# Moving ten loads of h from SyncE's queue to ScalarE's, and fetching two items ahead in place of five

## The chip, the cores and the metric

The kernel runs on one core of one Trainium2 chip. The metric is device time in microseconds (us) from launch to end. Three runs of the kernel before took 3075.65, 3078.77 and 3074.86 us, so the median is 3075.65 us. Engines are named as in the profile: PE is TensorE (matmuls; PEld its weight loads), DVE is VectorE, ACT is ScalarE, POOL is GpSimd, SP is SyncE. SPq, ACTq and POOLq are the queues on which those engines issue DMAs.

## The reference

Two graph attention layers over N = 2708 nodes with 1024 features, everything in float32; `adj` is an N x N matrix of 0 and 1.

```python
# layer 0
h = relu(layernorm(x))
f = h @ Wf + bf;  g = h @ Wg + bg
e = relu(f @ g.T)
attention = softmax(where(adj > 0, e, -9e15), axis=1)
x = x + attention @ (h @ W + bW)
# layer 1
h = relu(layernorm(x)); hh = h @ W1
e = leaky_relu(hh @ a1 + (hh @ a2).T)
attention = softmax(where(adj > 0, e, -9e15), axis=1)
x = x + relu(attention @ hh)
```

The case concerns layer 0 alone: the score product f @ g.T (the "scores"), and the rows of h that multiply the attention afterwards.

## The kernel before, in words

**Tiling.** The 2708 rows are cut into tiles of 128; 20 of them are worked on as ten pairs, 0 to 9, and a leftover unit (one tile of 128 rows and one of 20). The columns of the score matrix are cut into five panels, p = 0 to 4. Each product of 2 x 2 blocks is done with seven block products instead of eight (Strassen's scheme as Winograd ordered it), named M1 to M7, on sums and differences of blocks.

**The stage around the change: the first scores** (`scores(0, B)`, line 1372). `B` holds the panel's right sides and stays in SBUF. For each pair q the left sides, made earlier, are read from DRAM in four loads of a tile named `As` (line 1391): call them A (for M1 and M6), B (M5, M2), C (M7, M3), each 512 KB, and D (M4), 256 KB. `load` (line 137) puts every one of them on SP's queue in program order. PE's order is M1(q), M4(q-1), M6(q), M5(q), M2(q), M7(q), M3(q), eight matmuls each; M4 of a pair comes after M1 of the next, because `last` runs as the next pair's `left_over`. After pair 9 come the leftover unit's products (lines 1475 and 1483), whose left sides are one `As` load from `hsl_d` (512 KB). Then the next panel's projection starts (`project_q(1)`, matmuls `qx`), from eight loads `hT<-hs_d`, two `hT<-hsl_d`, and the loads of `md`.

DVE empties PSUM between the products, in program order (`nc.hold`). M2, M3, M4 and M7 add onto banks that DVE must have read before.

**The work that is slid in** is a list, `later`. `behind(us)` (line 214) is called after each product and takes items from its front while there is credit. Before `one()` (line 204) runs an item, it calls the fetch of the first `ahead[0]` items in the list, so `ahead` says how many items early the loads start.

**The sums of h** (`sums_h`, line 371) are such items, two for each pair: `first` and `second` hold four DVE operations together (tile `hr`). A pair's fetch makes two loads `hr<-hg_d` of 512 KB each; `first` has the fetch. The sums are stored to `hg_d` by POOL's queue in three stores (512, 256 and 256 KB). They are put into the list at pair q = 8 of the first scores (line 1428). The items of pairs 0 to 3, and `first` of pair 4, run during the rest of the first scores; after the scores `sums_may` stops them until the projection's M1 is done (line 1728). The sums are wanted in layer 0's first aggregation, `attention @ h`.

**Buffers and queues.** `As`, `hr`, `md`, `hc` and the adjacency tiles `adj_i` all come from one pool of 12 buffers (`strm`, line 119). A new tile takes the buffer that was given back longest ago in program order, and its load waits on the queue until that buffer's last use is over: the end of a matmul, of a DVE operation, or, for an `hr` buffer, of the stores that read it. A queue is worked in order: a load that waits holds up all loads behind it. [...]

`by_scalar` (line 540) issues a load on ACT's queue; the kernel before uses it for the rows of W in `prepare_W` alone. The entry `"m"` of `got` is set by `take_max(0)`, in the projection after the first scores.

Of the kernel before, what the change touches and what calls it, by code (L numbers as in the profile page):

```python
# [57 lines left out]
def kernel(  # L58
# [69 lines left out]
    def stream(name, shape=(P, D), dt=FP):  # L128
        return strm.tile(list(shape), dt, tag="strm", name=name)

    def in_16(o, i):

        n = o.shape[0]
        k = n // 16 * 16
        return [(o, i)] if n in (k, 1) or not k or i.shape[0] != n else [(o[:k], i[:k]), (o[k:], i[k:])]

    def load(o, i):
        for a, b in in_16(o, i):
            tc.keep_in_program_order(nc.sync.dma_start(a, b))

    def store(o, i):
        for a, b in in_16(o, i):
            nc.gpsimd.dma_start(a, b)  # L143
# [13 lines left out]
    hg_d = [dram.tile([P, 7, len(g), W], FP, name=f"hg_d{i}") for i, g in enumerate(groups)]  # L157
# [40 lines left out]
    ahead = [5]  # L198
    spare, from_slots = [False], [False]

    def put(us, go, fetch=None, takes_psum=False, ready=None, to=later):
        to.append([us, fetch, go, takes_psum, ready])
# [18 lines left out]
    def held(f, *a):  # L221
        was, nc.hold = nc.hold, ("vector",)
        r = f(*a)
        nc.hold = was
        return r
# [52 lines left out]
    def add(o, a, b):  # L278
        nc.vector.tensor_tensor(o, a, b, OP.add)

    def sub(o, a, b):
        nc.vector.tensor_tensor(o, a, b, OP.subtract)
# [88 lines left out]
    def sums_h():  # L371

        def fetch(q, two):
            i, j = group_of[q]
            for m in (M1, M2):
                two.append(stream("hr", (P, 2, W)))
                load(two[-1], hg_d[i][:, m:m + 2, j])

        def first(q, two):
            (a0, a1), (b0, b1) = ((t[:, 0], t[:, 1]) for t in two)  # L380
            add(b1, a1, b1)
            sub(a1, a0, a1)

        def second(q, two):
            (a0, a1), (b0, b1) = ((t[:, 0], t[:, 1]) for t in two)
            sub(a0, b1, a0)
            sub(b0, b0, a0)
            i, j = group_of[q]
            store(hg_d[i][:, M6:M7 + 1, j], two[0])
            store(hg_d[i][:, M3, j], b0)  # L390
            store(hg_d[i][:, M5, j], b1)
            summed[0] += 1
        for q in range(NQ):
            two = []
            put(1.4, lambda q=q, two=two: held(first, q, two), lambda q=q, two=two: fetch(q, two), ready=lambda: sums_may[0])
            put(1.4, lambda q=q, two=two: held(second, q, two), ready=lambda: sums_may[0])
# [956 lines left out]
    def once(q, k):  # L1353

        return NY if units[q][k] == TINY else P
# [16 lines left out]
    def scores(p, B):  # L1372

        w = width[p]
        h = w // 2
        lo, hi = slice(0, h), slice(h, w)
        fetch, convert, turn = makers[p]
        rb = slot("rb")
        if p == 0:
            spread(rb, columns_of(p, r_[:, first_col[p]:]))  # L1380
        else:
            row_on_all(rb, r_d[p], p)
        acc = slot("acc")
        S = [None] * NT
        rates = (0.8, 1.0, 0.65, 0.65, 0.65)
        lefts = {}

        def product(q, m, ps, start):
            n, i = P, BY_SCORES.index(m)
            if i % 2 == 0:  # L1390
                t = stream("As", (P, 2, NH, P))
                lefts[q] = t
                k = min(2, 7 - i)
                load(t[:, :k].rearrange("p m c j -> p (m c j)"),
                     hs_d[q][:, i:i + k].rearrange("p m c j -> p (m c j)"))
            for c in range(NH):
                nc.tensor.matmul(ps[:n, :h], lefts[q][:, i % 2, c, :n], B[m][c // 2][:, c % 2, :h],  # L1397
                                 start=(start and c == 0), stop=(c == NH - 1), skip_group_check=True)

        def finish(q, s, k):  # L1400

            n, mk = once(q, k), mk_sb[p, q]
            nc.vector.scalar_tensor_tensor(s[:, :w], s[:, :w], 0.0, mk[:, k, :w], op0=OP.max, op1=OP.add)
            if q == 0 and k == 0:
                nc.vector.tensor_copy(acc[:, :w], s[:, :w])
            else:
                nc.vector.tensor_tensor(acc[:n, :w], acc[:n, :w], s[:n, :w], OP.max)
            if q in known:
                raise_max(p, q, k, mk[:n, k, :w])

        def last(q, sb, Z, m1):

            n = P
            product(q, M4, Z, False)
            add(sb[:n, lo], Z[:n, :h], m1[:n, lo])
            finish(q, sb, 1)
            mk_sb.pop((p, q))
            behind(rate, True)

        nc.hold = ("vector",)  # L1420
        left_over = None
        for q in range(NQ):
            n = P
            make_until(q + 2)
            rate = 1.3 if NQ - 1 not in made else rates[p]
            if q + 2 <= LEFT:
                fetch(q + 2)
            if p == 0 and q == NQ - 2:
                sums_h()
            if p in ORDERED and q in (2, 6):  # L1430
                (copy_residual if q == 2 else bias_residual)(p)
            sa, sb = slot("Sa"), slot("Sb")
            S[pairs[q][0]], S[pairs[q][1]] = sa, sb
            X, Y, Z = (bank(f"s{k}") for k in "xyz")
            m1, t = slot("sm1"), slot("st")
            product(q, M1, X, True)
            for s in (lo, hi):
                add(m1[:n, s], X[:n, :h], rb[:n, s])
            if left_over:
                left_over()  # L1440
            product(q, M6, Z, True)
            add(t[:n, lo], Z[:n, :h], m1[:n, hi])
            behind(rate, True)
            product(q, M5, Y, True)
            add(t[:n, hi], Y[:n, :h], m1[:n, hi])
            if q + 1 <= LEFT:
                convert(q + 1, p > 0)
            behind(rate, True)
            product(q, M2, X, False)
            add(sa[:n, lo], X[:n, :h], rb[:n, lo])  # L1450
            if q + 1 <= LEFT:
                turn(q + 1, 0)
            behind(rate, True)
            product(q, M7, Z, False)
            add(sb[:n, hi], Z[:n, :h], t[:n, hi])
            if q + 1 <= LEFT:
                turn(q + 1, 1)
            behind(rate, True)
            product(q, M3, Y, False)
            add(sa[:n, hi], Y[:n, :h], t[:n, lo])  # L1460
            finish(q, sa, 0)
            behind(2 * rate, True)
            left_over = lambda q=q, sb=sb, Z=Z, m1=m1: last(q, sb, Z, m1)

        sums_may[0] = False
        sm, st = slot("Sa"), slot("Sb")
        S[MONO], S[TINY] = sm, st
        X, Y, Z = (bank(f"s{k}") for k in "xyz")
        m1, zs = slot("sm1"), slot("sz")
        t = stream("As", (P, 2, NH, P))  # L1470
        load(t.rearrange("p e c j -> p (e c j)"), hsl_d.rearrange("p e c j -> p (e c j)"))

        def part(ps, e, m, start):
            for c in range(NH):
                nc.tensor.matmul(ps[:, :h], t[:, e, c], B[m][c // 2][:, c % 2, :h], start=(start and c == 0),
                                 stop=(c == NH - 1), skip_group_check=True)
        part(X, 0, M1, True)
        add(m1[:, hi], X[:, :h], rb[:, hi])
        left_over()

        for c in range(NH):
            for g, (e, m) in enumerate(((0, M1), (1, M2), (0, M5), (1, M3))):
                nc.tensor.matmul(Z[B32 * g:B32 * (g + 1), :h], tinyT[:, e, c], B[m][c // 2][:, c % 2, :h], start=(c == 0),
                                 stop=(c == NH - 1), skip_group_check=True)
        nc.scalar.copy(zs[:, :h], Z[:, :h])
        part(X, 1, M2, False)
        add(sm[:, lo], X[:, :h], rb[:, lo])
        behind(rate, True)
        part(Y, 0, M5, True)
        part(Y, 1, M3, False)  # L1490
        add(sm[:, hi], Y[:, :h], m1[:, hi])
        finish(LEFT, sm, 0)
        for s, pick in zip((lo, hi), picks):
            V = bank("sv")
            nc.tensor.matmul(V[:, :h], pick, zs[:, :h], start=True, stop=True)
            add(st[:, s], V[:, :h], rb[:, s])
        finish(LEFT, st, 1)
        mk_sb.pop((p, LEFT))
        behind(rate, True)
        nc.hold = ()  # L1500
        return S, acc
# [189 lines left out]
    got = {}  # L1691
# [205 lines left out]
```

## Time and profile before

| | us |
|---|---|
| median of three runs | 3075.65 |
| the profiled execution's own time | 3071.02 |
| its span | 3069.2 |
| PE busy | 2999.9 (98%) |
| DVE busy | 2042.9 (67%) |
| ACT busy | 546.1 (18%) |
| first scores, from pair 8's M5 to the first matmul of the projection | 340.68 to 391.14 |

The profile page gives busy time by engine, DMA by queue, the chain of work that ended last, and groups of equal instructions. The trace behind it answers for any stretch of time: an engine's instructions in order with what ended the idle time before them, the issues on a DMA queue, and busy time, clock and DMA share by stretches. All times in the span are counted from its start.

### The profile page before, as it was taken

The page shows a single profiled execution, that of the slowest core. Times are in us where ns is not written, and L with a number is a line of the kernel's source. Part 1 is how long each engine was busy: PE and PEld are TensorE (multiplying, and loading weights), DVE is VectorE, ACT ScalarE, POOL GpSimd, SP SyncE. Part 2 cuts the span into 40 slices and gives each one's busy share as a digit, 9 for nine tenths or more (in the row PEclk, how much of TensorE's full clock was granted, in tenths as well). Part 3 has the DMA queues.
Part 4 walks back from the last instruction along what each step waited for, and adds up shares of the span by engine and source line. Part 5 has one row for each costly group of instructions (what it writes and reads, how often), then busy time and mean ns, then how long its engine had stood idle before and what let it go on. Part 6 is the DMA issues. An engine that isn't in the chain of part 4 may idle for free.

```text
span 3069.2 us, 41688 instructions
## 1 busy us (share of the span) xinstructions
PE 2999.9 (98%) x14630; PEld 2298.9 (75%) x14630; DVE 2042.9 (67%) x4577; ACT 546.1 (18%) x887; POOL 496.0 (16%) x770
## 2 busy tenths in 40 slices
PE   8998899999999999999999999998999999999999
PEld 4576677757877588885888887784767969879695
DVE  5776694676651586715965266967868767887863
ACT  3420020021110121101211011202222121222200
POOL 1421101210011110214102011131212011020201
PEclk9999999999999999999999999998999999999999
DMA  6989868897565786758967588689767868878897
GB/s 227 301 258 274 291 239 294 275 291 222 178 234 152 228 254 221 247 154 238 280 216 250 165 234 264 230 293 332 240 212 249 274 201 302 279 271 295 259 300 270
DMA packets 448065, 766.80 MB, mean 250 GB/s; under 512 B 175488, under 2 KB 262304, under 8 KB 447824
## 3 DMA queue, kind: packets, MB, share of 16 engines
q1 hardware_dynamic: 390416, 590.05, 60.2%
q0 software_dynamic: 54464, 164.78, 16.1%
q10 hardware_dynamic: 2976, 9.31, 0.9%
q8 instruction: 116, 1.90, 0.2%
q14 instruction: 93, 0.76, 0.1%
HBM read 630.04 MB, written 138.11 MB: 250 GB/s over the span
## 4 chain that ended last, share of the span: by engine, by line
PE 75%; DVE 9%; issue 7%; DMA 6%; POOL 1%; SPq 1%; ACT 1%; POOLq 0%; DVEq 0%; ACTq 0%
PE gy L673 7%; PE sz L1397 7%; PE gz L673 7%; PE gx L673 6%; PE gz L1086 5%; PE sx L1397 4%; PE sy L1397 4%; PE px L1286 4%; PE pz L1286 4%; PE py L1286 3%; PE gx L1086 3%; PE gy L1086 3%; PE gv L673 3%; PE M_ps L586 3%; PE qz L673 2%
## 5 line engine op out<-in xcount | busy, mean ns | idle before, releaser
L1397 PE MATMUL sz<-B,As 128*128 128x288 f32 (+2 forms) x1200 | 294.3, 395 | 5.9 <-DVE st L45 4.5
L1397 PEld LDWEIGHTS sz<-B,As 128*128 128x128 f32 x1200 | 229.1, 192 | 56.6 <-DVE st L45 8.2
L1397 PE MATMUL sx<-B,As 128*128 128x288 f32 (+2 forms) x800 | 203.6, 398 | 16.5 <-DMA As<-hs_d 14.6
L1397 PE MATMUL sy<-B,As 128*128 128x288 f32 (+2 forms) x800 | 199.0, 392 | 0.0
L1397 PEld LDWEIGHTS sx<-B,As 128*128 128x128 f32 x800 | 153.5, 193 | 51.2 <-DMA As<-hs_d 12.9
L673 PE MATMUL gz<-Sa,hc 128*128 128x288 f32 (+2 forms) x800 | 185.8, 392 | 0.0
L673 PEld LDWEIGHTS gz<-Sa,hc 128*128 128x128 f32 x800 | 151.5, 190 | 32.2 <-issue 2.2
L1397 PEld LDWEIGHTS sy<-B,As 128*128 128x128 f32 x800 | 151.7, 190 | 30.6 <-DVE st L45 0.3
L1086 PE MATMUL gz<-quarter,hc 128*128 128x128 f32 (+2 forms) x1344 | 168.8, 279 | 3.8 <-DVE gT L45 3.7
L1086 PEld LDWEIGHTS gz<-quarter,hc 128*128 128x128 f32 x1344 | 160.6, 191 | 5.1 <-DVE gT L45 4.6
L143 POOL DMA_DIRECT2D out_dram<-x_res x164 | 80.9, 500 | 467.2 <-DVE x_res L45 456.6
L1286 PE MATMUL px<-w,gT 128*128 128x512 f32 x320 | 141.2, 593 | 1.5 <-ACT pt L45 1.5
L1286 PE MATMUL py<-w,ps 128*128 128x512 f32 x320 | 142.2, 593 | 0.0
L1286 PE MATMUL pz<-w,ps 128*128 128x512 f32 x320 | 142.1, 594 | 0.0
L143 POOL DMA_DIRECT2D mk_d<-mask x55 | 35.9, 653 | 510.7 <-DVE mask L45 504.8
L673 PE MATMUL gy<-T,hc 128*128 128x288 f32 (+2 forms) x480 | 113.6, 398 | 3.9 <-DMA hc<-hg_d 3.9
L1286 PEld LDWEIGHTS pz<-w,ps 128*128 128x128 f32 x320 | 60.2, 190 | 76.2 <-issue 70.3
L1286 PEld LDWEIGHTS py<-w,ps 128*128 128x128 f32 x320 | 60.5, 190 | 75.1 <-issue 72.0
L1286 PEld LDWEIGHTS px<-w,gT 128*128 128x128 f32 x320 | 60.1, 190 | 72.9 <-issue 66.9
L586 PE MATMUL M_ps<-wgT,wfT 128*128 128x512 f32 x256 | 111.8, 593 | 1.6 <-ACT hsT L45 1.6
L673 PEld LDWEIGHTS gy<-T,hc 128*128 128x128 f32 x480 | 92.2, 192 | 24.4 <-DMA hc<-hg_d 4.4
L45 ACT ACTIVATE P<-P 128x576 f32<-128x576 f32 (+2 forms) x110 | 71.9, 654 | 207.6 <-DVE P L45 207.5
(384 smaller groups left out, 5829.1 us busy)
## 6 DMA issues: line engine op xcount, KB each, us to landing
hc<-hg_d SPq DMA_DIRECT2D x175, 512.0 KB
As<-hs_d SPq DMA_DIRECT2D x150, 512.0 KB
hc<-hr_d SPq DMA_DIRECT2D x119, 512.0 KB
hc<-hs_d SPq DMA_DIRECT2D x112, 512.0 KB
w<-wt_d SPq DMA_DIRECT2D x96, 512.0 KB
w<-in_L_gnn_W_dram SPq DMA_DIRECT2D x72, 512.0 KB
md<-md_d SPq DMA_DIRECT2D x56, 512.0 KB
adj_i<-in_adj_dram SPq DMA_DIRECT2D x200, 128.0 KB
```

Of the source, the lines that this page charges most:

```text
L45: i = f(*a, **k)
L143: nc.gpsimd.dma_start(a, b)
L586: nc.tensor.matmul(ps, wfT[a][c // NH][:, c % NH, :], wgT[b][c], start=(c == 0), stop=(c == NC - 1))
L673: nc.tensor.matmul(ps[d], left(m, k, d), right(m, k), start=(start and k == 0), stop=(k == K - 1), skip_group_check=True)
L1086: nc.tensor.matmul(ps[:, d], lhs[:, d * P:(d + 1) * P], inner_right(m, n, k), start=(start and k == 0 and d == 0), stop=(k == NK - 1), ski ...
L1286: nc.tensor.matmul(ps, left[i][m][:, k, :], w_[k], start=(start and k == 0), stop=(k == NH - 1), skip_group_check=True)
L1397: nc.tensor.matmul(ps[:n, :h], lefts[q][:, i % 2, c, :n], B[m][c // 2][:, c % 2, :h], start=(start and c == 0), stop=(c == NH - 1), skip_g ...
```

## The change

Two edits. In `sums_h` the loads of `hr` go through `by_scalar` as long as `"m"` is not in `got`, and through `load` after that. And `ahead` is set to 2 where the sums are put into the list; it was 5 until the end of the first scores, where the kernel before sets it to 2 as well.

```diff
@@ def sums_h(): def fetch(q, two):
             for m in (M1, M2):
                 two.append(stream("hr", (P, 2, W)))
-                load(two[-1], hg_d[i][:, m:m + 2, j])
+                (load if "m" in got else by_scalar)(two[-1], hg_d[i][:, m:m + 2, j])
@@ def scores(p, B):
             if p == 0 and q == NQ - 2:
+                ahead[0] = 2
                 sums_h()
```

In the built kernel, ten of the twenty `hr` loads (pairs 0 to 4) are issued by ACT; they stand after the last copies `hsT<-h_ps` and ahead of the copy `sz<-sz` of the leftover unit. The other ten stay with SP. Before, SP's queue held the `hr` loads of pairs 0 to 6 among the `As` loads of pairs 8 and 9; now it holds none there, and those of pairs 5 to 7 stand together after the projection's first four `md` loads, where before only those of pair 7 stood. Fewer `hr` loads ahead also means that other buffers of the pool come round for the `As` loads. The order of instructions on PE, DVE and POOL is the same in both kernels.

## The prediction

> **What bounds the kernel now.** I began with the page: PE carries the time, so only what keeps PE waiting or slow counts.
>
> ```profile
> PE 2999.9 (98%) x14630; PEld 2298.9 (75%) x14630; DVE 2042.9 (67%) x4577; ACT 546.1 (18%) x887; POOL 496.0 (16%) x770
> ```
>
> Next I took the stage of the change in stretches of 5 us (PE busy, PEld, DVE, ACT, POOL, PE clock, DMA share, GB/s).
>
> ```profile
> 335.00:340.00 5.00, 5.00 (x23) 3.90 (x22) 3.73 (x7) 0.00 (x0) 0.16 (x1) 1.00 0.70 249
> 345.00:350.00 5.00, 3.99 (x16) 2.96 (x16) 4.42 (x11) 0.00 (x0) 0.82 (x2) 1.00 0.68 238
> 350.00:355.00 5.00, 0.13 (x1) 0.00 (x0) 3.87 (x6) 0.00 (x0) 2.09 (x4) 0.87 1.00 313
> 355.00:360.00 5.00, 4.70 (x10) 3.41 (x11) 0.46 (x2) 0.00 (x0) 0.00 (x0) 0.50 1.00 394
> 370.00:375.00 5.00, 1.70 (x7) 0.98 (x6) 4.86 (x10) 0.00 (x0) 1.82 (x3) 0.91 1.00 374
> 375.00:380.00 5.00, 4.70 (x10) 3.42 (x11) 1.03 (x2) 0.00 (x0) 0.54 (x1) 0.50 1.10 370
> 395.00:400.00 5.00, 5.00 (x25) 3.99 (x24) 3.63 (x8) 1.20 (x3) 0.00 (x0) 1.00 0.16 22
> ```
>
> PE nearly stops twice, and runs at half clock after each stop. The chain of work (start, us) says for what:
>
> ```profile
> 340.87 5.00 DMA As<-hs_d
> 346.01 2.19 PE sz L1397 x8
> 348.91 6.34 DMA As<-hs_d
> 355.30 4.21 PE sx L1397 x8
> ...
> 367.85 7.41 DMA As<-hsl_d
> ...
> 375.30 4.21 PE sx L1475 x8
> 379.51 2.73 PE sz L1397 x8
> ```
>
> Three `As` loads come late: C of pair 8, A of pair 9, the leftover's. SP's queue in the same stretch shows why they were issued late:
>
> ```profile
> 347.88 0.94 SPq L139 DMA_DIRECT2D hr<-hg_d  x2
> 348.91 1.68 SPq L139 DMA_DIRECT2D As<-hs_d  x3
> 359.52 2.88 SPq L139 DMA_DIRECT2D hr<-hg_d  x2
> 362.50 0.41 SPq L139 DMA_DIRECT2D As<-hs_d  x1
> 363.97 3.40 SPq L139 DMA_DIRECT2D hr<-hg_d  x2
> 367.85 0.52 SPq L139 DMA_DIRECT2D As<-hsl_d  x1
> ```
>
> Ahead of each stand `hr` loads that wait for buffers; SP's waits from 300 to 480 by what ended them (us in all, times, the longest) say which:
>
> ```profile
> SPq L139 <- DMA hg_d<-hr: 48.2, 14, 8.9
> ```
>
> So the queue stood for stores of finished sums.
>
> The loss: eight matmuls take 1.94 us from start to start here. From 340.68 to 391.14 lie 16 such groups, the leftover's small products (2.07) and four picks (0.97): 34.1 us of work in 50.5, so **16.4 us lost**. Group by group: 1.45 before 346.01, 5.34 before 355.30, 3.77 before 375.30, and 5.8 in slowed matmuls (4.00 for 1.94 twice, the rest just after).
>
> [...] the clock is 0.50 after the stops of 5.17 and 3.60 us, and after one of 1.29 the eight matmuls take 2.18. [...] the share is 1.00 with SP and POOL issuing. [...]
>
> **The change, part by part.**
>
> *Removed:* fourteen `hr` loads from among the `As` loads on SP. Each took about 0.36 us to issue, which is nothing; what counted was their waiting.
>
> *Added:* ten `hr` loads on ACT, 0.33 us each by the rows of W that ACT's queue already loads. ACT stood idle for 127.4 us until 384.38, and behind them is only the copy `sz<-sz`, after the last `hr` load's condition (M4 of pair 8) by 15 us of products. Cost: 0. Without that idle time it would be 3.3 us plus the waits.
>
> *Moved:* four `hr` loads (pairs 5 and 6) now go out after the first scores: 2 MB less in the crowded stretch, about 5.5 us at the 370 GB/s seen when full. They wait on SP ahead of `md` for the third product, but that `md` waits for the projection's M1 to end anyway. The last of these loads waits for the end of the leftover's products, T (the projection's start); six loads of 0.5 MB are 8.5 us of transfer, begun about 7 us before T, landing by about T+5. DVE wants pair 5 at about T+11.5 (402.7 against 391.1). Hidden with 6 us to spare; beyond those, each us late is a us of DVE, which is busy all of 410 to 450.
>
> [...]
>
> *Walking PE without stalls*, from the built kernel's waits (the load's condition, the time by the row before, and when PE wants it):
> - A of 9: M4 of pair 7 ends at 338.7, lands by 345, wanted 348.4.
> - D of 8: M6 of 8, 340.7, lands by 346, wanted 350.4.
> - B of 9: now waits for pair 0's store of 512 KB. That store was done at 347.87 before (the `hr` load behind it went out then). Two ACT loads now run beside it from 344.6, 1 MB, at half share: 1 to 1.5 us later, 349.0. Landing takes 5.0 to 6.34: 354.0 to 355.4, wanted 354.3. I take **0.7 late**.
> - C of 9: right behind it, lands by 357.5, wanted 358.1. In time.
> - Leftover: waits for pair 1's store. Before, issued at about 350.9, done at 359.5. The bytes in 348.5 to 357.5 are about as many (3.3 MB against 3.1), but the `hr` loads are now on another queue; I take 357.6 to 358. Landing 5.0 to 6.3: 363.5, wanted 362.0 plus the 0.7. **0.8 late**.
> - D of 9: just behind, wanted 1.9 later still. In time.
> - `hT` and `md`: before, from the first `hT` issue (371.64) to the last of the four `md` issues is 13.5 us, and about 4 to land (3.93 by a quiet `md`): 17. From 358.7 that is 376; PE wants them at 374.8 plus 1.5. I take **0.8 late** as the midpoint of 0 and 1.6.
>
> *DVE under a PE that doesn't stall:* pair 8 with six sums operations extra carries about 15.2 us of DVE work in a 13.6 us period. It falls about 3.5 us behind by 357.5. PE wants M6's bank read 3.9 us after M6 ends, so this just fits. With 0.4 us to spare I count 0, with 1 us in the range.
>
> Sum: 16.4 - 0.7 - 0.8 - 0.8 = **14.1 us gained**. [...] On the profiled execution: 3071.02 - 14.1 = 3056.9; it lies 4.63 below the median, so the forecast is **3061.6**. After T, PE has one wait on DMA (3.9 us, `hc<-hg_d`), which hangs on DVE and stores that shift with T, so nothing gives the gain back.
>
> **Rivals.**
> 1. *Stores gate the leftover* (one real stop stays). The slowest rows: pair 1's store done at 359.5, landing 7.41 us: 366.9, so 4.9 late, plus 3.1 of half clock, plus 1.4 for B of 9. Loss 9.4, gain 7.0: 3068.7. For: DMA share 1.00. Against: less to move.
> 2. *DMA is the limit, whichever queue.* Before T about 12.7 MB must move from 338.8 on (`As` 2.5, `hr` 2, stores of sums 4.2, masks 0.9, `hT` 2.2, `md` 1). At the 322 GB/s mean of 340 to 390 that is 39.4 us, 378.2 against 374.8: gain 13. At 254 GB/s, 50 us and nothing is gained: about 3075. The 228 to 246 GB/s of 280 to 320 speak for it, but those hold the small adjacency pieces, which end at 322.
> 3. *Slower:* [...] each `As` load lands as late as the slowest row of W on ACT's queue, 11.3 us (median 7.9). A of 9 is 1.7 late, B of 9 4.3 more and 2.9 of clock, the leftover (pair 1's store as late again) 3.4 and 3.1, `hT` and `md` about 4: 19.4 lost, 3 more than now. It decides from about 10.5 us of landing; at 13, some 9 us slower: 3084. Against: 0.5 MB takes 5.0 to 7.4 here with as much beside it.
> 4. *It doesn't do what it says:* ten of twenty loads only are moved. But those are all that stand among the `As` loads, so this is not a case of its own.
>
> **How the numbers follow.** The likeliest case (gain 10 to 16.4) 0.66; rival 1 (5 to 10) 0.16; rival 2 (within 5) 0.12; rival 3 0.06. A measurement of this kernel tells about 0.2%, 6.2 us. Faster by more is the first and most of the second, 0.81; within 0.13; slower 0.06. The range takes the first two cases: from 3057.5 (all of 16.4, and 1.8 for the runs' spread) to 3070.5.
>
> **What would show it.** Right: ACT's queue holds ten `hr` loads between 323 and 353; no wait of PE above 2 us and no clock of 0.50 between 340 and T; T near 377 in place of 391.14; DVE's run of ten `hr` operations starts about 11 us after T, as before. Wrong: `As<-hsl_d` issued after 360, or landing in over 7 us; a clock of 0.50; `hr` waits of DVE after T; T earlier, but a new wait of PE before 500.

## The result, and the profile after

The kernel after takes **3064.88 us** (median of 6 runs, 3062.58 to 3065.96); the kernel before took 3075.28 us beside it (6 runs, 3070.99 to 3079.16). The comparison gives a ratio of 0.9956 with a 95% interval of 0.9947 to 0.9966; the quotient of the two medians is 0.9966, a gain of 10.4 us. The forecast was 3061.6 with a range of 3057.5 to 3070.5.

On the profile page PE is still the engine that carries the time, with 7.3 us less than before:

```profile
PE 2992.6 (98%) x14630; PEld 2293.3 (75%) x14630; DVE 2041.7 (67%) x4577; ACT 546.0 (18%) x887; POOL 496.2 (16%) x770
```

The stage of the change in stretches of 5 us (the columns are as before: PE, PEld, DVE, ACT and POOL busy, clock, DMA share, GB/s):

```profile
340.00:345.00 5.00, 5.00 (x22) 3.95 (x21) 3.96 (x6) 0.00 (x0) 0.54 (x1) 1.00 0.53 168
350.00:355.00 5.00, 5.00 (x22) 3.90 (x21) 4.86 (x9) 0.00 (x0) 1.94 (x4) 1.00 1.02 365
355.00:360.00 5.00, 4.57 (x19) 3.32 (x18) 4.90 (x11) 0.00 (x0) 1.53 (x3) 1.00 1.01 383
365.00:370.00 5.00, 2.46 (x10) 1.99 (x11) 4.02 (x7) 0.00 (x0) 1.98 (x4) 1.00 1.05 351
375.00:380.00 5.00, 5.00 (x22) 3.94 (x21) 0.64 (x2) 0.00 (x0) 0.00 (x0) 1.00 1.12 348
```

The clock is 1.00 in every stretch, and one stretch is left in which PE does half of what it could. PE's timeline names its stop (start, us, what, and in brackets the idle time before and what ended it):

```profile
342.64 2.10 PE L1397 MATMUL sy<-B,As 128*128 128x288 f32 x8
...
356.81 2.21 PE L1397 MATMUL sy<-B,As 128*128 128x288 f32 x8 [0.43 <-DMA As<-hs_d]
...
367.54 2.21 PE L1476 MATMUL sx<-B,As 128*128 128x288 f32 x8 [2.70 <-DMA As<-hsl_d]
...
380.59 7.92 PE L673 MATMUL qx<-hT,md 128*128 128x288 f32 x32
```

342.64 is M5 of pair 8 and 380.59 the projection's start, T. The stage takes 37.95 us in place of 50.46. C of pair 8 and A of pair 9 are on time; B of 9 and the leftover's load are late by 0.43 and 2.70 us. SP's queue and ACT's in the same stretch:

```profile
323.90 26.73 SPq L139 DMA_DIRECT2D As<-hs_d  x8
360.83 0.32 SPq L139 DMA_DIRECT2D As<-hsl_d  x1
361.77 0.32 SPq L139 DMA_DIRECT2D As<-hs_d  x1
362.14 10.82 SPq L139 DMA_DIRECT2D hT<-hs_d  x8
373.00 2.01 SPq L139 DMA_DIRECT2D hT<-hsl_d  x2
375.12 2.53 SPq L139 DMA_DIRECT2D md<-md_d  x4
377.77 4.58 SPq L139 DMA_DIRECT2D hr<-hg_d  x6
```

```profile
322.27 32.61 ACTq L45 DMA_DIRECT2D hr<-hg_d  x10
```

No `hr` load stands among the `As` loads any more. Yet SP's waits from 300 to 480, by what ended them (us in all, times, the longest), hardly differ from the 48.2 us in 14 waits of before:

```profile
SPq L139 <- DMA hg_d<-hr: 44.8, 14, 10.1
```

SP stands for stores nearly as long; the longest of these waits is now that of `As<-hsl_d` itself. That the waiting stayed and the time went was the first hint that the queue was not the matter.

### The profile page after: what moved, and what is told of

Same layout as the page of the kernel before. It is cut to its first block, busy times and chain, and to the rows that moved or that the text cites. A ratio compares the mean times of both kernels' runs of the same rounds, so it can differ in the third digit from the quotient of the medians.

```text
span 3060.8 us, 41690 instructions
## 1 busy us (share of the span) xinstructions
PE 2992.6 (98%) x14630; PEld 2293.3 (75%) x14630; DVE 2041.7 (67%) x4577; ACT 546.0 (18%) x887; POOL 496.2 (16%) x770
## 4 chain that ended last, share of the span: by engine, by line
PE 71%; issue 11%; DVE 9%; DMA 4%; POOL 2%; SPq 1%; ACT 1%; POOLq 0%; DVEq 0%; ACTq 0%
PE gy L673 7%; PE gx L673 6%; PE gz L673 6%; PE sz L1397 6%; PE gz L1086 5%; PE pz L1286 4%; PE px L1286 4%; PE sx L1397 4%; PE sy L1397 3%; PE py L1286 3%; PE gy L1086 3%; PE gx L1086 3%; PE M_ps L586 3%; PE gv L673 2%; PE qz L673 2%
## 5 line engine op out<-in xcount | busy, mean ns | idle before, releaser
L1397 PEld LDWEIGHTS sx<-B,As 128*128 128x128 f32 x800 | 152.4, 191 | 48.4 <-DMA As<-hs_d 10.4
```

## The experiments

Every kernel has the same order of matmuls but for one place in `all_slots`, so one reading serves all: the *head* up to M5 of pair 8, the *stage* from there to T, and the *tail* from T to the end of the span, all from PE's timeline.

| run | head | stage | tail | median us (runs) | ratio to before [95%] |
|---|---|---|---|---|---|
| before | 340.68 | 50.46 | 2678.06 | | |
| before_look | 346.62 | 50.40 | 2680.38 | one run | |
| after | 342.64 | 37.95 | 2680.21 | 3064.88 (6) | 0.9956 [0.9947, 0.9966] |
| again | 343.87 | 39.24 | 2677.89 | 3065.59 (7) | 0.9972 [0.9961, 0.9983] |
| again2 | 348.52 | 39.27 | 2678.91 | 3068.45 (5) | 0.9958 [0.9946, 0.9971] |
| queue_only | 345.37 | 49.05 | 2679.78 | 3072.95 (13) | 0.9998 [0.9990, 1.0007] |
| ahead_only | 345.95 | 38.87 | 2679.08 | 3064.14 (6) | 0.9969 [0.9958, 0.9981] |
| left_slots | 344.95 | 36.80 | 2680.15 | 3063.70 (5) | 0.9962 [0.9950, 0.9975] |
| pool16_before | 342.94 | 40.00 | 2702.76 | 3089.14 (5) | 1.0043 [1.0028, 1.0057] |
| pool14_after | 338.12 | 34.67 | 2697.01 | 3069.32 (19) | 0.9980 [0.9973, 0.9987] |
| act_all | 346.91 | 40.85 | 2694.04 | 3076.55 (12) | 1.0005 [0.9996, 1.0013] |
| ahead3 | 343.48 | 42.78 | 2682.64 | 3070.59 (9) | 0.9971 [0.9961, 0.9981] |
| ahead1 | 350.89 | 38.55 | 2682.46 | 3072.30 (6) | 0.9972 [0.9961, 0.9983] |
| all_slots | 343.85 | 38.84 | 2680.21 | 3064.68 (5) | 0.9951 [0.9937, 0.9964] |

The kernel before took 3073.24 us beside again, queue_only, ahead_only and left_slots (20 runs), 3075.32 beside before_look, pool16_before, pool14_after and act_all (32), and 3080.96 beside the last four (15); so times compare only within a group, stages across all. The head spreads over 13 us, and over 10 us without the two pool kernels, in which alone the program differs long before the head ends; that is about the spread of single times of the kernel before (3069.19 to 3081.10 in the 32 runs).

**Each edit alone.** The two edits of the change, one at a time, and the whole change again.

```diff
# queue_only
-                load(two[-1], hg_d[i][:, m:m + 2, j])
+                (load if "m" in got else by_scalar)(two[-1], hg_d[i][:, m:m + 2, j])
# ahead_only
             if p == 0 and q == NQ - 2:
+                ahead[0] = 2
                 sums_h()
```

> The changed kernel once more, for a closer interval and a second profile. By the walk corrected with its first profile (stage from pair 8's M5 to the projection 37.95 us against 50.46) it is 12.5 us faster than before; by the medians of its first runs 10.4. If the 2 us between them are given back later in the kernel, the stage is again 12 to 13 us shorter and the whole only 10; if they are spread from elsewhere, the two agree within 2 us over more runs. The leftover's As load again waits for pair 1's store and PE for it by 2 to 4 us.

> Only the first edit: hr loads by ACT's queue, still five items ahead. Theory (two causes: the queue's order, and how many hr tiles hold buffers): the hr loads no longer stand before the As loads, but six hr tiles still hold half of the pool, so As loads themselves wait for the stores of sums: D of pair 8 for pair 0's, C of pair 9 for pair 1's, D of pair 9 for pair 2's. About 1.4 late for C of 8, 0.8 for A of 9, 2.5, 3 and 1 for those three: 9 us lost of which before lost 16.4, so a gain of 4 to 8 us (about 3070). Rival (the queue alone is the cause): nearly the whole gain of the change, 9 to 13 us, and no As load issued within 0.5 us of a store's landing.

> Only the second edit: two items ahead, all hr loads still on SP. Theory: this is the larger part. Two hr loads (pairs 3 and 4) still stand before As loads, the last of them waiting for pair 1's store with the leftover's As load behind it, so that load goes out at the same time as in the changed kernel (about 18 us after pair 8's M5 began) and lands 0 to 1.5 us later behind 0.5 MB more on its own queue. A gain of 8 to 12 us (3063 to 3067), at most 3 short of the whole change. Rival (the queue alone is the cause): a gain under 4 us.

The whole change repeats, but the stage of again is 11.2 us shorter than before, not 12 to 13: after its stop of 3.00 us the next two groups of eight matmuls took 2.89 and 2.88 us from start to start in place of 1.94. The edit of `ahead` alone gives all of it, with every `hr` load still on SP. The edit of the queue alone gives nothing clear of the noise: the interval holds 1, and the 4 to 8 us that I expected of it were wrong. PE's timeline of queue_only:

```profile
350.12 2.18 PE L1397 MATMUL sz<-B,As 128*128 128x288 f32 x8 [0.71 <-DMA As<-hs_d]
...
357.20 2.21 PE L1397 MATMUL sx<-B,As 128*128 128x288 f32 x8 [2.96 <-DMA As<-hs_d]
362.34 5.81 PE L1397 MATMUL sz<-B,As 128*128 128x288 f32 x16 [2.93 <-DMA As<-hs_d]
...
379.69 3.90 PE L1475 MATMUL sx<-B,As 128*128 128x288 f32 x8 [3.78 <-DMA As<-hsl_d]
```

and its two queues, SP's first, then ACT's, and two rows of what SP waited for from 300 to 480 us (us in all, times, the longest):

```profile
323.10 41.37 SPq L139 DMA_DIRECT2D As<-hs_d  x8
372.05 0.32 SPq L139 DMA_DIRECT2D As<-hsl_d  x1
```

```profile
321.82 49.76 ACTq L45 DMA_DIRECT2D hr<-hg_d  x14
```

```profile
SPq L139 <- PE sx L1397: 15.9, 4, 7.4
SPq L139 <- PE sz L1397: 9.3, 1, 9.3
```

The fourteen `hr` loads are off SP's queue, and the eight `As` loads still take 41.37 us to go out, against 26.73 in the kernel after. The `As` loads' own conditions say why. When each went out, in us from the start of M5 of pair 8, and what ended its wait, from the traces:

| load | before | queue_only | its wait in queue_only ended with | after | its wait in after ended with |
|---|---|---|---|---|---|
| C of 8 | 0.2 | 0.2 | M6 of 8 | -10.4 | DVE (an adjacency tile) |
| A of 9 | 8.2 | 4.1 | M2 of 8 | -1.8 | M4 of 7 |
| D of 8 | 8.8 | 10.2 | a store of pair 0 | 0.2 | M6 of 8 |
| B of 9 | 9.5 | 10.6 | (behind D of 8) | 5.8 | a store of pair 0 |
| C of 9 | 21.8 | 18.8 | a store of pair 1 | 7.7 | a store of pair 0 |
| leftover | 27.2 | 26.7 | M2 of 9 | 18.2 | a store of pair 1 |
| D of 9 | 30.6 | 29.6 | a store of pair 2 | 19.1 | a store of pair 1 |

PE stops in queue_only for C of 8, A of 9, D of 8 and the leftover's load. Only one of these, D of 8, waited for a store. The other three were dealt the buffer of an `As` tile used just before: M6 is the last product that reads A of its pair, M2 the last that reads B. So such a load can go out only two products, 3.9 us, before it is wanted itself. With fourteen `hr` tiles fetched early from a pool of 12, so few buffers are left that an `As` load takes over that of the `As` tile two or three loads before it. With ten, C of 8 and A of 9 meet buffers that came free earlier, and so does the leftover's load, though that one waits for a store.

**Buffers, bytes or queue.** The kernel before, its queue and its loads untouched, with four more buffers in the pool; and once more as it is, to see whether the 50.46 repeats.

```diff
# pool16_before
-    slots = ctx.enter_context(tc.tile_pool(name="slots", bufs=54))
-    strm = ctx.enter_context(tc.tile_pool(name="strm", bufs=12))
+    slots = ctx.enter_context(tc.tile_pool(name="slots", bufs=47))
+    strm = ctx.enter_context(tc.tile_pool(name="strm", bufs=16))
```

> The kernel before, once more. The stage is counted from pair 8's M5 to the first matmul of the next projection; the head is what lies before it, the tail what lies after it to the end of the span. If the program repeats itself, the stage takes 49.5 to 51.5 us (50.46 in the first profile) with the same three stops, for C of pair 8, A of pair 9 and the leftover; the head lies in 340 to 346 and the tail in 2677.5 to 2680.5, where those of all profiles so far lie. If the 50.46 was an accident of one run, the stage comes out below 45 us and the whole comparison of stages falls.

> The kernel before (all loads on SyncE, five items ahead, so the same bytes and the same queue), with the streaming pool at 16 buffers in place of 12 and 47 slots in place of 54. With four more buffers the As loads of pairs 8 and 9 meet buffers that matmuls and DVE give back, except B of 9 (pair 0's store) and the leftover (behind an hr load that waits for pair 1's store): the same two conditions as in the changed kernel. My theory now (buffers, not the queue and not the bytes): no stop at C of 8 or A of 9, the stage falls from 50.5 to 38 to 42 us, and the kernel is 8 to 12 us faster than before, 3063 to 3067, with ten hr loads still on SyncE. Rival, bandwidth: the 2 MB that the changed kernel leaves out of the stretch are what counts; here they are still in it, so the stage stays at 45 us or more and the gain is under 6 us. Rival, the queue of SyncE itself: as before, stage 49 to 51 us, no gain.

The stage repeats at 50.40 (only the head, 346.62, lies past what I gave it). With 16 buffers it takes 40.00. PE's timeline of pool16_before has these stops and no others in the stage:

```profile
363.37 3.71 PE L1397 MATMUL sz<-B,As 128*128 128x288 f32 x8 [2.80 <-DMA As<-hs_d]
...
369.90 2.21 PE L1475 MATMUL sx<-B,As 128*128 128x288 f32 x8 [0.88 <-DMA As<-hsl_d]
```

and its SP queue still holds the `hr` loads in the midst of the `As` loads:

```profile
334.70 2.97 SPq L139 DMA_DIRECT2D hr<-hg_d  x2
341.20 9.84 SPq L139 DMA_DIRECT2D As<-hs_d  x3
351.30 0.88 SPq L139 DMA_DIRECT2D hr<-hg_d  x2
352.29 0.41 SPq L139 DMA_DIRECT2D As<-hs_d  x1
353.12 8.69 SPq L139 DMA_DIRECT2D hr<-hg_d  x2
361.92 0.45 SPq L139 DMA_DIRECT2D As<-hsl_d  x1
```

So 10.4 of the 11.6 us that the change saves in the stage (mean of after, again and again2: 38.8) come with more buffers alone, the queue as it was and nearly all of the bytes: from 20.6 us ahead of the stage to T, 21.1 MB are moved here, 22.1 in the kernel before and 19.0 in the kernel after. The forecast of the total, 8 to 12 us faster, failed all the same: the tail grew by 22 us or more (from 1200 to 2400 PE is busy 1163 us, against 1182 in the kernel before). My reading is that the stages after T miss the seven tiles that the other pool gave up; no run takes these away by themselves. That does not touch the reading of the stage.

**Taking the last stop away.** Four ways to free the leftover's load from pair 1's store: its left sides in tiles of the other pool (left_slots); those and two loads of pair 9 (all_slots); 14 buffers in the pool (pool14_after); three items ahead, which happens to deal the leftover a buffer that a matmul gives back (ahead3). The last edit has its counterpart in ahead1.

```diff
# left_slots (all_slots does the same for B and D of pair 9)
-        t = stream("As", (P, 2, NH, P))
-        load(t.rearrange("p e c j -> p (e c j)"), hsl_d.rearrange("p e c j -> p (e c j)"))
+        if p == 0:
+            sides = [slot("Asl", (P, NH, P)) for _ in range(2)]
+            for e in range(2):
+                load(sides[e].rearrange("p c j -> p (c j)"), hsl_d[:, e].rearrange("p c j -> p (c j)"))
...
# pool14_after
-    slots = ctx.enter_context(tc.tile_pool(name="slots", bufs=54))
-    strm = ctx.enter_context(tc.tile_pool(name="strm", bufs=12))
+    slots = ctx.enter_context(tc.tile_pool(name="slots", bufs=51))
+    strm = ctx.enter_context(tc.tile_pool(name="strm", bufs=14))
# ahead3
-                ahead[0] = 2
+                ahead[0] = 3
                 sums_h()
# ahead1
-                ahead[0] = 2
+                ahead[0] = 1
                 sums_h()
```

> The changed kernel, with the leftover's left sides in two tiles of the other pool (slots) for the first panel, so that their loads wait for no store. Theory (the 2.7 us wait of PE is the store that gates the load, not DMA bandwidth): the load goes out 9 to 10 us earlier, right behind C of pair 9, and PE's wait for the leftover goes; D of pair 9 keeps the gate and may be up to 1 us late. 2 to 3 us faster than the changed kernel, about 14 to 15 faster than before. Rival (bandwidth): the same bytes move in the same time, so the wait returns at D of pair 9 or at the projection's first hT or md, and the time is that of the changed kernel within 1 us.

> The changed kernel with 14 streaming buffers and 51 slots. No As load of pairs 8, 9 or the leftover waits for a store any more; only matmuls and DVE give their buffers back, and two hr loads on ScalarE wait for pair 0's stores. Theory (stores that hold buffers are all that is left to gain): the wait of 2.7 to 3.0 us before the leftover's products goes, the stage takes 34.5 to 36.5 us against 38.0 and 39.2, and the kernel is 2 to 4 us faster than the changed one, 3060 to 3063. Rival, bandwidth: the loads go out earlier and land slower, the wait comes back at the projection's first matmul (1 to 3 us), and the time stays at 3063 to 3066.

> The changed kernel with three loads for pair 9 and the leftover (B and D of 9, the leftover's left sides) read into tiles of the other pool, each split in two, so that none of them waits for a store; C of 9 waits for pair 0's stores. Sizes of both pools as they were. Theory: stage 34.5 to 36.5 us, the kernel 1.5 to 4 us faster than the changed one on this chip, as long as the tiles taken from the other pool make nothing wait elsewhere (the part after T stays within 2677.5 to 2680.5). Rival, bandwidth: the earlier loads collide, and 1 to 3 us come back at the projection's first matmul.

> The changed kernel with three items ahead in place of two. Twelve hr loads then go to ScalarE and eight to SyncE, 1 MB more is read ahead of the projection, and the pool comes round otherwise: the leftover's load waits for the end of M6 of pair 9, some ten us ahead of the leftover's products, not for pair 1's store; D of 9 for a product too; of the As loads only B of 9 still waits for a store (pair 0's first). Theory (what counts is which loads take over buffers that stores hold): the wait of 2.7 to 3.0 us before the leftover's products goes although more is read, the stage from pair 8's M5 to the projection takes 34.5 to 37 us, and the kernel is 1 to 3 us faster than the changed one on this chip. Rival (fewer hr loads ahead is what helps, by their bytes): three lies between five and two, the stage takes 40 to 45 us and the kernel is 2 to 5 us slower than the changed one.

> The changed kernel with one item ahead in place of two. Ten hr loads on ScalarE still, but they start later. By the buffers, C of 9 waits for pair 0's stores and the leftover's load and D of 9 for pair 1's, much as in the changed kernel. Theory: the leftover is late as before by 2 to 4 us, the sums' operands may come late on DVE (under 2 us each), the stage takes 37.5 to 42 us and the kernel is within 3 us of the changed one, on the slower side. Rival (fewer bytes ahead help): stage below 37 us, 1 to 3 us faster than the changed one.

> The changed kernel once more, on the chip of the three runs beside it: stage 37.5 to 40 us, part after T 2677.5 to 2680.5, time 8 to 12 us below the kernel before on the same chip. It is the measure for the other three, nothing else.

The leftover's wait goes in all of left_slots, all_slots, pool14_after and ahead3. In left_slots 1.25 us return at D of 9, which still waits for pair 1's store, and 0.85 at the projection; the stage is 2.4 us shorter than that of again. In pool14_after nothing takes its place; the stage is 34.67 us, within 0.6 of the 34.1 of pure work. Its PE timeline around T:

```profile
371.93 0.65 PE L1496 MATMUL sv<-sz,pick_hi 128*128 128x288 f32 x2
372.79 8.37 PE L673 MATMUL qx<-hT,md 128*128 128x288 f32 x32 [0.21 <-issue]
```

But with three tiles less in the other pool the tail is 17 to 19 us longer, and by its ratio the kernel gains less than the changed one. In all_slots C of 9 is 0.40 us late, PE waits 0.98 us for DVE where the order of products differs, and the projection's `hT` and `md` are late, as the rival said:

```profile
379.34 0.65 PE L1507 MATMUL sv<-sz,pick_hi 128*128 128x288 f32 x2
382.69 8.00 PE L673 MATMUL qx<-hT,md 128*128 128x288 f32 x32 [2.70 <-issue]
```

("issue" here: this view names no releaser; by the trace the first `md` load, out at 377.63, landed at 382.60.) In ahead3 my forecast fell, and stage and time are those of the rival. A of 9 is late, and the projection too:

```profile
345.42 2.10 PE L1397 MATMUL sx<-B,As 128*128 128x288 f32 x8
...
353.44 3.90 PE L1397 MATMUL sx<-B,As 128*128 128x288 f32 x8 [2.04 <-DMA As<-hs_d]
...
386.26 9.84 PE L673 MATMUL qx<-hT,md 128*128 128x288 f32 x32 [3.19 <-issue]
```

But the first of these stops is not one of bytes. A of 9 went out at 347.55, right when M2 of pair 8 (345.42, above) had ended, and landed in 5.9 us: as in queue_only it was dealt the buffer of B of 8. I had looked for stores alone. For the projection, `hT` stands on the queue behind D of 9, which went out at 365.12 when M2 of 9 had ended, and the `hT` loads then took 12.67 us to go out, 10.82 in the kernel after. How much of the 3.19 us is crowding, no run separates. With twelve early `hr` loads in place of ten, the DMA share is higher where the kernel after leaves room:

```profile
340.00:350.00 10.00, 10.00 (x43) 7.82 (x42) 8.69 (x17) 0.00 (x0) 2.37 (x4) 1.00 1.05 400
```

400 GB/s at a share of 1.05 from 340 to 350, against 212 at 0.64 in the kernel after. Yet pool16_before moves as much to T (21.1 MB, 20.9 here) in a stage 2.8 us shorter. Where the leftover's load is early (left_slots, all_slots), part of the stop returns at the projection. That the transfers crowd each other there is my reading; no run takes bytes away there alone. By their medians left_slots and all_slots lie 1.9 and 3.8 us below the changed kernel on their chips; their intervals overlap its, so no version is shown to beat it. ahead1 stays close to the changed kernel in the stage (38.55, leftover 2.40 and projection 1.26 late), so fewer bytes ahead did not help as its rival had it. It is 3.9 us slower by its median, of which about 3 us lie in the tail; why there, I did not look for.

**Without the cover for the moved loads.** The prediction held six `hr` loads after T to be hidden. Here all twenty go to ACT, and those of pairs 5 to 7 then stand behind ACT's evictions of the projection.

```diff
-                (load if "m" in got else by_scalar)(two[-1], hg_d[i][:, m:m + 2, j])
+                by_scalar(two[-1], hg_d[i][:, m:m + 2, j])
```

> The changed kernel with all twenty hr loads on ScalarE. Those of pairs 5 to 7 then stand among ScalarE's evictions of the projection, behind its first one (some 9 us after T, the projection's start), where on SyncE they were issued by about T + 2. The prediction called the loads of pairs 5 and 6 hidden with 6 us to spare. If that margin is right, pair 5's operations on DVE begin 2 to 6 us later than T + 10.5 and DVE, busy there, ends its sums that much later; TensorE loses 0 to 3 us in the projection, and the kernel takes 3065 to 3068, still 7 us below the kernel before. If the margin is larger than I thought, nothing changes (3063 to 3066). If the waits on ScalarE's queue hold up the evictions that TensorE needs, over 3 us are lost: 3069 or more. The stage before T is as in the changed kernel, 37 to 40 us, in every case.

The loads go out some 13 us later, counted from T (from T + 10.6, where the kernel after has T - 2.8). The timelines of act_all: ACT's queue, DVE, and PE.

```profile
398.35 2.19 ACTq L45 DMA_DIRECT2D hr<-hg_d  x4
402.17 1.00 ACTq L45 DMA_DIRECT2D hr<-hg_d  x2
```

```profile
406.59 0.69 DVE L45 TENSOR_TENSOR hr<-hr 128x512 f32<-128x512 f32 x1 [7.60 <-DMA hr<-hg_d]
...
417.44 0.69 DVE L45 TENSOR_TENSOR hr<-hr 128x512 f32<-128x512 f32 x1 [3.03 <-DMA hr<-hg_d]
```

```profile
444.93 10.20 PE L673 MATMUL qz<-hT,md 128*128 128x288 f32 x32 [7.23 <-DVE B L45]
```

(The kernel after has ten `hr` operations in one run at 391.13, T + 10.5.) The margin lay near where I thought: the loads are 13.4 us later and DVE waits 7.6 for pair 5, so 5.8 were to spare, but 7.6 is past the 2 to 6 expected. The price did not: DVE stands 10.6 us in all, PE 8.1 for DVE (this stop and one of 0.88) and then runs slowed (10.20 us for the 32 matmuls, 8.01 for the 32 before them; clock 0.66 from 440 to 450), and the tail is 14 us or more longer, against 0 to 3 expected. The profiled run is the slowest of the twelve, 7.0 us above their median. The third of my branches, waits worth over 3 us, came about by another road than ACT's evictions. The stage was to stay at 37 to 40 us and took 40.85: a stop of 3.40 at the leftover, and slowed matmuls after it (4.21 us for eight; clock 0.66 from 370 to 380). The whole gain is gone. In this program SP's place behind the first `md` loads is needed.

## Why the prediction was right, and where it was not

- *Removed:* "what counted was their waiting". This is the step that failed: queue_only takes the `hr` loads off SP's queue and keeps 49.05 us. Of the three late loads in the kernel before, only A of 9 (348.91) stood behind an `hr` load that waited for a store, until 347.88. C of 8 went out at 340.87 and the leftover's load at 367.85, each right at the end of the product that gave its own buffer back, M6 of 8 and M2 of 9. PE's timeline of the kernel before (M6 of 8 is the second half of the first row):

```profile
336.80 4.04 PE L1397 MATMUL sz<-B,As 128*128 128x288 f32 x16
...
365.71 2.10 PE L1397 MATMUL sx<-B,As 128*128 128x288 f32 x8
```

The forecast came near because the walk used the load conditions of the built kernel after, where these buffers come free earlier; the sentence about the cause named the wrong part of the change. The edit that does it is the one of `ahead`, which I booked under "moved" and "2 MB less".
- *Added:* ten loads on ACT at no cost: right. They went out from 322.27 in 32.61 us, and ACT's next work, the copy of `sz`, came at 373.83 when its product was there.
- *Moved:* hidden, right (377.77 to 382.35; DVE starts at T + 10.5 as predicted). act_all shows what the margin is worth.
- *B of 9:* 0.7 predicted, 0.59 measured (plus 0.1 in its matmuls). That is luck: two errors cancelled. Counted from M5 of pair 8, pair 0's store was done 1.4 us sooner than in the kernel before (it took 3.1 us, from 345.29 to 348.38), not 1 to 1.5 later (the half share behind that figure was an estimate, and the trace does not show it); and B of 9 took 8.3 us to land (348.43 to 356.77), not 5.0 to 6.34. Times of landing here are those recorded in the trace.
- *C and D of 9:* in time, right. But C was not right behind B: another store of pair 0 held it until 350.32, and it landed after 9.7 us, 0.8 us before PE wanted it.
- *The leftover:* 0.8 predicted; 2.86 measured; the bare stop is 2.70 there, 3.00 in again and 3.23 in again2. This is the term that was mis-sized. POOL issued pair 1's store of 512 KB at 351.60, and the load that waits for it went out at 360.83: 9.2 us. In the kernel before the same store took as long, 350.30 to 359.46; I had put its issue at 350.9, and then let it shrink to about 7 because `hr` loads were on another queue. It did not shrink (9.1 and 9.5 us in again and again2). Landing took 6.7 us, just above the 5.0 to 6.3. That is rival 1's mechanism at less than half its price. That the other queue would shorten it was an estimate, and the runs do not show it: the store takes 9.2 us with the `hr` loads on either queue, with the DMA share at 1.00 from 350 to 360 in the kernel before and at 1.01 to 1.03 from 350 to 365 in the kernel after.
- *The clock:* 1.00 all through the stage in after, with its stop of 2.70 us. But in again the stop of 3.00 us and in again2 that of 3.23 were followed by slowed matmuls, some 1.9 and 1.6 us more (clock 0.79 from 370 to 375 in again2). That stops of this length leave the clock as it is was not shown.
- *hT and md:* 0.8 predicted, none measured. *DVE* kept up; PE waits for it nowhere in the stage.
- *Nothing is given back:* right; tails of 2677.9 to 2680.2 against 2678.1 and 2680.4.

Sum: 16.4 lost before, 3.8 after in the profiled run where 2.3 was forecast, and about 5 in again and again2. So the stage gave 12.5, 11.2 and 11.2 us in place of 14.1. The medians differ by 10.4, 7.7 and 12.5 us on the three chips. Of the 3.3 us between forecast and result, 1.6 to 2.9 are this shortfall; the rest is less than single times spread. Of the signs of being right one failed: PE had a wait above 2 us, the 2.70. Counted from M5 of pair 8, T came 1.6 us after the 377 named.

Rival 2, bandwidth, is refuted as the cause of the old loss (pool16_before moves 21.1 of the 22.1 MB in a stage of 40.0); as the limit of what is left it is likely, not shown. Rival 3 did not come, but was nearer than I thought: it was to decide from about 10.5 us of landing, and in the kernel after B and C of 9 took 8.3 and 9.7, against the 5.0 to 7.4 that I had set against it.

## What to carry to other kernels

Where tiles of several kinds share one rotating pool, look not only at what stands ahead of a late load on its queue, but at which buffer the load itself is dealt and what gives that buffer back, and when: it can be the product just before the one that wants the load, or a store for its whole flight. Fetching less far ahead can speed up the loads that matter, because early tiles leave the others fewer buffers. Moving the early fetch to another queue leaves that as it is. And before enlarging the pool, look at what the other pool loses: here four more buffers won 10 us in one stage and lost 22 in the others.

## What the runs showed of the hardware

- **Two stores of 512 KB took 3.1 and 9.2 us.** In the kernel after, pair 0's took 3.1 us (from 345.29; the DMA share is 0.76 from 345 to 350), and pair 1's, from 351.60 with the share at 1.01 to 1.03, held the leftover's load for 9.2 us.
- **The length of a stop alone does not tell whether slowed matmuls follow.** Eight matmuls take 2.10 us where no stop is ahead of them (lines above). They took 3.90 us after a stop of 2.04 (ahead3, lines above), 3.71 after 2.80 (pool16_before) and 3.09 after 3.00 (again), but 2.21 after 2.70 (after), 2.96 (queue_only) and 3.14 (ahead_only). What decides it, these runs do not show. The profile's clock in the two stretches of ahead3 around its first stop:

```profile
350.00:355.00 5.00, 2.96 (x10) 1.90 (x9) 4.90 (x11) 0.00 (x0) 1.82 (x3) 0.86 0.96 346
355.00:360.00 5.00, 5.00 (x18) 3.80 (x17) 2.59 (x6) 0.00 (x0) 0.54 (x1) 0.80 1.02 383
```

What stays open: why the head varies by 13 us from run to run, why ahead1 and ahead3 have tails some 3 us longer, and in all_slots why the `hT` loads, issued from 357.54 on, took 18.29 us to go out where the kernel after needed 10.82. Of that, the third waited 2.3 us, until 361.75, when C of 9 had landed after 10.3 us; that the third and fourth then took 4.2 and 4.7 us each to issue is not explained.
